# A two-layer relational graph attention kernel: float32 key products and twelve row buffers in the preparation, query numbers of 16 groups gathered by GpSimd

## The chip, the cores and the metric

The kernel runs on one core of a Trainium2 chip. The metric is the device time of one execution in microseconds (us); lower is better. The engines are TensorE (PE; PEld is its weight load), VectorE (DVE), ScalarE (ACT), GpSimd (POOL) and SyncE (SP, which here only issues DMAs). Each engine works through its own row of instructions in order, and DMAs can be issued from SP, ACT and POOL.

## What is computed

Two layers of relational graph attention, a residual and a layer norm. There are 3125 nodes of 768 features, 53125 edges sorted by destination, and 3 relations.

```python
def rgat_conv(x, W, q, k, b, src, dst, etype, heads, out_ch, n_nodes):
    xr = jnp.einsum('nd,rdf->rnf', x, W)
    oi = xr[etype, dst]
    oj = xr[etype, src]
    qi = oi @ q
    kj = oj @ k
    alpha = jax.nn.leaky_relu(qi + kj, NEG_SLOPE)
    m = jax.ops.segment_max(alpha, dst, num_segments=n_nodes)
    e = jnp.exp(alpha - m[dst])
    z = jax.ops.segment_sum(e, dst, num_segments=n_nodes)
    a = e / (z[dst] + EPS)
    msg = (a[:, :, None] * oj.reshape(-1, heads, out_ch)).reshape(-1, heads * out_ch)
    out = jax.ops.segment_sum(msg, dst, num_segments=n_nodes)
    return out + b
...
h = jax.nn.elu(rgat_conv(x, W1, q1, k1, b1, ...))    # 4 heads of 192
out = layernorm(x + rgat_conv(h, W2, q2, k2, b2, ...))   # 1 head of 768
```

An edge's score needs two numbers a head: the key number of its source row and the query number of its destination row, both for the edge's relation. `W @ k` and `W @ q` give columns that are carried along with W, so that one product of x with the widened W yields rows, key numbers and query numbers.

## The kernel before

The 3125 nodes are 25 blocks of 128. The edges are 25 groups: a group holds the edges of up to 128 consecutive destination nodes, in up to 17 slots of 128 edges (14 in the first).

There are four stages, and in each an order written out by hand: a table of steps (`when(n, f, ...)`) lists which function emits its instructions at which step, and every engine's row follows from it.

*The preparation* (`weights_kq`, psum0 and work0). W1 is loaded as 18 rows of 128 features ("W" 0 to 17, six a relation); each is split into a high half (ACT, L378) and a low half (POOL, or DVE for every third, L379), since the big products take a high and a low half of each factor. For the key and query columns each W row is also needed transposed: for relation 0, PE transposes it (L56); for relations 1 and 2 a transposed copy is loaded ("T" rows, two per pair of W rows). The transposes are split into halves too (tH by ACT, L389; tL by DVE, L390). For each pair m = 0 to 8 of W rows, `product(m)` multiplies them with `kqs` (12 matmuls in `times`), ACT copies the result (sm, L402), PE turns it back, and `place` (DVE: L410, L412, and L416 and L417 twice each) writes the columns into the widened weights `waH`, `waL`, `wbH`, `wbL`. Row buffers are handed out by `Buffers`: seven of them, and the next load on SP's row waits until the oldest is free. The edge lists are loaded by ACT and written to DRAM by POOL meanwhile (`prepare`, driven by `more`).

A *piece* is one of 150 products of phase 1's kind: 18 matmuls of a block of x (its halves `xT`) with 386 or 398 columns of the widened weights, into one bank, which ACT copies (L581) and SP stores into the table `tab1`. Each block has six pieces. Pieces 0 to 7 are emitted inside the preparation, between the products of relations 1 and 2; piece 8 is the first of phase 1.

*Phase 1* (`phase1`, psum1 and work1) has the other 142 pieces, one a step, from step 2 on (step n is piece n + 6). Beside them it prepares each group's edges, loads and halves the blocks of x, splits W2 (its rows loaded on POOL's row, L745, into one shared row), and computes each group's query numbers `pall`: `s_load1` loads the group's destination numbers to all partitions (SP), `q_load1` the block's query numbers as three bfloat16 parts (SP), `a_q` and `a_oh` compare (DVE), `a_q2` picks by 17 small matmuls (PE), `a_q3` multiplies and sums (DVE). For the last four groups this stands after the last piece.

*Phase 2* gathers each slot's rows of `tab1` (POOL, L468), forms scores, maxima and weighted sums, and makes the second table; it reads `pall`. *Phase 3* does the second layer and the layer norm.

Of the kernel before, what the change touches and what calls it, by code (L numbers as in the profile page):

```python
# [109 lines left out]
def kernel(  # L110
# [54 lines left out]
    xb_d = dram.tile([NP + P, D], F32, name="xb_d")  # L165
    q1_d = dram.tile([NP + P, H1 * R * 3], BF, name="q1_d")
    w2_d = dram.tile([R * DT * P, 2 * D], F32, name="w2_d")

# [45 lines left out]
    class Buffers:  # L214


        def __init__(self):
# [4 lines left out]
            self.spare = list(range(6)) + [7]  # L222
            self.at = {}
            self.go()

        def __getitem__(self, key):
            return share[self.at[key]][:, :D]

# [120 lines left out]
    def weights_kq(buf, work, psum, kqr, kqs, split, piece, rows_out, more):  # L349

        V.memset(kqs.bitcast(F32), 0.0)
        kq = kqr.rearrange("p t s h -> p t (s h)")
        V.tensor_copy(kqs[:, :, 0:8], kq)
        V.tensor_sub(kqs[:, :, 8:16], kq, kqs[:, :, 0:8].bitcast(F32))

# [7 lines left out]
        def turn(m):  # L363
            r, t = divmod(2 * m, DT)
            made = parts[m] = []
            if r == 0:
                for i in range(2):
# [5 lines left out]
                    made.append(pt)  # L373
            for c in range(2):
                i = 2 * m + c
                hi, lo = (w[:, :, :F1] for w in heads(t + c, r))
                own = buf["W", i].rearrange("p (h f) -> p h f", h=H1)
                S.copy(hi, own)  # L378
                (V if i % 3 == 2 else G).tensor_sub(lo, own, hi.bitcast(F32))  # L379
                buf.free("W", i)  # L380
            for i in range(2):
                hi, lo = (work.tile([P, DT // 2, 2 * P], F32R, name=f"t{n}", bufs=4) for n in "HL")
                if r == 0:
                    to = [t.rearrange("p f (c n) -> p c f n", c=2) for t in (hi, lo)]
                    raw = made[i][:, :, :DT // 2 * P].rearrange("p c (f n) -> p c f n", f=DT // 2)
                else:
                    to = hi, lo
                    raw = buf["T", 2 * m + i].rearrange("p (f n) -> p f n", f=DT // 2)
                S.copy(to[0], raw)  # L389
                V.tensor_sub(to[1], raw, to[0].bitcast(F32))  # L390
                if r > 0:
                    buf.free("T", 2 * m + i)
                made[i:i + 1] = [(hi, lo)]

        prod = {}

        def product(m):
            r, t = divmod(2 * m, DT)
            pk = psum.tile([P, 512], F32, name="bank", bufs=2)[:, :2 * P]
            times(pk, kqs, parts.pop(m))  # L400
            sm = work.tile([P, 2 * P], F32, name="sm", bufs=2)
            S.copy(sm[:16], pk[:16, :2 * P])  # L402
            prod[m] = r, t, sm

        def place(r, t, sm):
            pb = psum.tile([P, 2, 512], F32, name="pt", bufs=2)[:, 0, :]
            for c in range(2):
                T.transpose(pb[:, c * 16:(c + 1) * 16], sm[:16, c * P:(c + 1) * P], ident[:16, :16])
            g = work.tile([P, 2, 16], F32, name="g16", bufs=2)
            V.tensor_copy(g, pb[:, :32].rearrange("p (c k) -> p c k", c=2))  # L410
            w = work.tile([P, 2, 8], F32, name="w8", bufs=2)
            V.tensor_add(w, g[:, :, 0:8], g[:, :, 8:16])  # L412
            k, o = divmod(r, WHOLE)
# [5 lines left out]
        def placed(m):  # L419
            place(*prod.pop(m))  # L420
# [11 lines left out]
        placed(1)  # L432
        split(0)
        placed(2)
        split(1)
        for r in range(1, R):
            m = 3 * r
            for j in range(4):
                piece()
                rows_out(1)  # L440
                if j < 3:
                    turn(m + j)
                if j > 0:
                    product(m + j - 1)
                if j > 1:
                    placed(m + j - 2)
                if r == 1:
                    more(1)
            placed(m + 2)

# [128 lines left out]
    def d_row(o, q, b, p, po):  # L579
# [4 lines left out]
        if p == len(PIECES1) - 1:  # L584
            q1s = q.tile([P, H1 * R, 3], BF, name="q1s", bufs=2)
            split3([q1s[:, :, i] for i in range(3)], po[:, HW:HW + H1 * R], q, [P, H1 * R])
            nc.sync.dma_start(q1_d[b * P:(b + 1) * P, :], q1s.rearrange("p k s -> p (k s)"))

    def stretches(rows, at_, a, e):
# [11 lines left out]
    def phase1(pre, work, psum, left, due, more):  # L601
# [14 lines left out]
        def a_index2(b):  # L616
# [7 lines left out]
            if b in first_rows:  # L624
                V.tensor_scalar(rfirst[:, first_rows[b], :], ridx[:, b, :], NP * R - 1, None, op0=ALU.min)
            V.tensor_copy(rel[:, b, :], pT[:, 2 * c:3 * c])

        counts = work.tile([32, 32], F32, name="counts", bufs=1)
# [54 lines left out]
        def a_oh(b):  # L683
            s = st[b]
            s["oh"] = work.tile([P, SL, R * 3], F32, name="oh", bufs=2)
            V.tensor_tensor(s["oh"], rel[:, b, :, None].to_broadcast([P, SL, R * 3]),
# [51 lines left out]
        def w_load(i):  # L738
# [5 lines left out]
            for p, at, n in feature_rows(t):  # L744
                G.dma_start(w2[i][p:p + n], l2["W"][r, at:at + n, :])  # L745

        def w_split(i):
# [10 lines left out]
            if r < WHOLE:  # L758
                (G if i >= 4 else nc.sync).dma_start(w2_d[i * P:(i + 1) * P, :].rearrange("p (s f) -> p s f", s=2), hl.bitcast(F32))

# [13 lines left out]
        S0 = 10  # L774
        when(8, pad_rows)
        for b in range(NB):
            c = S0 + 5 * b
# [22 lines left out]
        for i in range(R * DT):  # L800
            when(6 * (2 + i), w_load, i)
            when(6 * (2 + i) + 2, w_split, i)
        for p, (r, f, n) in enumerate(((0, 0, HW), (0, HW, D - HW), (1, 0, HW), (1, HW, D - HW))):
            when(TAIL + 4 * p + 5, second_weights, r, f, n)
# [726 lines left out]
    with tc.manual_schedule():  # L1531
        with tc.tile_pool(name="share", bufs=1) as pool:
# [5 lines left out]
            with tc.tile_pool(name="wbuf", bufs=1) as wbuf:  # L1538
                weights[0] = [wbuf.tile([P, DT, WA], F32R, name=f"wa{s}") for s in "HL"]
                with tc.tile_pool(name="wrest", bufs=1) as wrest, tc.tile_pool(name="pre", bufs=1) as pre:  # L1540
# [16 lines left out]
                    with tc.tile_pool(name="work0", bufs=1) as work, tc.tile_pool(  # L1557
                        name="psum0", bufs=1, space=PSUM
                    ) as psum:

                        buf = Buffers()
# [3 lines left out]
                        kqs = work.tile([P, DT, P], F32R, name="kqs")  # L1565
                        banks[:] = [psum.tile([P, 512], F32, name=f"po{i}") for i in range(2)]
# [572 lines left out]
```

## Time and profile before

| what | us |
|---|---|
| median of 3 runs | 1765.43 (1759.7 to 1765.5) |
| the profiled execution, its own time | 1765.7 |
| its span, first to last instruction | 1763.9 |
| start to the first piece | 20.96 |
| first piece to piece 8 (rest of the preparation) | 44.74 |
| phase 1 (142 pieces) | 465.1 |
| from there on (phases 2 and 3) | 1233.1 |

A row of the timeline is: start, length (both us), engine, line, operation, what it writes and reads, shapes, count if equal instructions were put together, and in brackets the idle time before it and what ended that. A row of groups is: line, engine, operation, tiles, shapes, count, then busy us and mean ns of one, then idle time before. "SPq" and "ACTq" are DMA issues on these engines' rows.

### The profile page before, as it was taken

To read this page: it belongs to the slowest core of one execution; us is meant where nothing else is said; L and a number is where in the kernel's file an instruction comes from. 1 tells how busy PE (TensorE), PEld (TensorE's weight loads), DVE (VectorE), ACT (ScalarE), POOL (GpSimd) and SP (SyncE) were. 2 spreads that over 40 slices of the span, in tenths; PEclk is the share of its full clock that TensorE was granted. 3 is DMA by queue.
4 is the path that set the end of the run, shared out by engine and by line. 5 is a ranking of instruction groups with operands and counts; after the bars stand their busy time and mean duration, and the time that the engine had idled before them with its cause. 6 is when DMAs were issued, how large, how long until landed. Compare 5 with 4: busy or idle time off the path is not lost. (4 is left out here: it accounts for less than half of the span.)

```text
span 1763.9 us, 38699 instructions
## 1 busy us (share of the span) xinstructions
PE 1648.9 (93%) x14093; PEld 1282.5 (73%) x14093; DVE 1116.9 (63%) x3911; ACT 438.0 (25%) x805; POOL 901.3 (51%) x907
## 2 busy tenths in 40 slices
PE   8999999999993899999999999939999999999996
PEld 8999999999992688888888888825444444444443
DVE  7566667566525666666677777455666666666663
ACT  6222222211210122121221112212333333333331
POOL 4100000000006777777777777057777777777760
PEclk9999999999996899999999999969999999999998
DMA  8576766656577999999999999469999999999970
GB/s 271 177 243 218 217 224 231 199 171 209 187 266 266 322 350 359 354 349 348 347 345 347 342 349 343 131 218 317 340 339 335 341 336 334 337 337 341 340 274 20
DMA packets 169367, 501.55 MB, mean 284 GB/s; under 512 B 39890, under 2 KB 82489, under 8 KB 169166
## 3 DMA queue, kind: packets, MB, share of 16 engines
q0 software_dynamic: 70832, 343.91, 55.1%
q1 hardware_dynamic: 90104, 144.97, 24.8%
q10 hardware_dynamic: 8230, 10.10, 1.7%
q8 instruction: 113, 1.85, 0.4%
q14 instruction: 88, 0.72, 0.1%
HBM read 414.04 MB, written 89.63 MB: 286 GB/s over the span
## 5 line engine op out<-in xcount | busy, mean ns | idle before, releaser
L468 POOL DMA_INDIRECT extra<-ftab,ridx x296 | 301.6, 1019 | 94.4 <-issue 52.7
L53 PE MATMUL po<-waH,hT 128*128 128x386 f32 (+1 forms) x1200 | 326.2, 346 | 1.4 <-DVE hT L1031 0.7
L53 PE MATMUL po<-waH,xT 128*128 128x386 f32 x1104 | 294.6, 343 | 0.9 <-ACT xT L255 0.4
L468 POOL DMA_INDIRECT share<-ftab,ridx x209 | 211.5, 1012 | 68.9 <-issue 41.0
L53 PEld LDWEIGHTS po<-waH,hT 128*128 128x128 f32 x1200 | 216.6, 189 | 4.8 <-DVE hT L1031 1.1
L53 PE MATMUL D<-extra,AT 128*128 128x256 f32 (+1 forms) x600 | 211.4, 504 | 5.3 <-ACT AT L1399 5.3
L53 PEld LDWEIGHTS po<-waH,xT 128*128 128x128 f32 x1104 | 203.9, 190 | 1.4 <-DVE xT L256 0.8
L53 PE MATMUL po<-waL,hT 128*128 128x386 f32 (+1 forms) x600 | 203.0, 338 | 0.0
L53 PE MATMUL po<-waL,xT 128*128 128x386 f32 x552 | 188.3, 341 | 3.1 <-DVE wbH L416 3.0
L53 PEld LDWEIGHTS D<-extra,AT 128*128 128x128 f32 x600 | 113.9, 196 | 69.6 <-issue 48.3
L581 ACT COPY share<-po 128x386 f32<-128x386 f32 x150 | 72.3, 482 | 368.9 <-PE po L53 296.4
L53 PE MATMUL acc<-waL,marks 128*32 128x386 f32 (+1 forms) x860 | 151.9, 489 | 0.0
L53 PE MATMUL po<-wbH,xT 128*128 128x386 f32 (+1 forms) x552 | 147.5, 341 | 0.9 <-DVE g L410 0.9
L53 PE MATMUL acc<-waH,marks 128*32 128x384 f32 (+1 forms) x828 | 140.4, 493 | 0.7 <-DVE marks L1321 0.7
L53 PE MATMUL acc<-extra,marks 128*32 128x386 f32 (+1 forms) x564 | 129.5, 487 | 0.0
L468 POOL DMA_INDIRECT waL<-ftab,ridx x108 | 107.9, 999 | 33.6 <-issue 25.3
L53 PE MATMUL acc<-extra,sel 128*32 128x193 f32 x2736 | 122.9, 332 | 2.3 <-DVE sel L940 2.3
L468 POOL DMA_INDIRECT waH<-ftab,ridx x103 | 103.7, 1007 | 31.4 <-issue 25.3
L53 PEld LDWEIGHTS po<-waL,hT 128*128 128x128 f32 x600 | 113.3, 189 | 0.0
L53 PE MATMUL acc<-share,marks 128*32 128x384 f32 (+1 forms) x456 | 109.7, 487 | 0.0
L745 POOL DMA_DIRECT2D share<-in_L_gnn_W_dram x24 | 12.8, 538 | 188.5 <-DVE w2j L756 117.1
L53 PEld LDWEIGHTS acc<-extra,sel 128*32 128x32 f32 x2736 | 86.5, 111 | 30.4 <-issue 4.9
(286 smaller groups left out, 2990.9 us busy)
## 6 DMA issues: line engine op xcount, KB each, us to landing
ftab<-share SPq DMA_DIRECT2D x150, 193.0 KB
ftab<-r SPq DMA_DIRECT2D x50, 386.0 KB
sT<-dr_d SPq DMA_DIRECT2D x23, 544.0 KB
xb_d<-share SPq DMA_DIRECT2D x25, 384.0 KB
ftab<-y SPq DMA_DIRECT2D x100, 96.0 KB
share<-xb_d SPq DMA_DIRECT2D x25, 384.0 KB
share<-in_x_dram SPq DMA_DIRECT2D x24, 384.0 KB
out_dram<-share SPq DMA_DIRECT2D x24, 384.0 KB
```

Source lines behind the costliest of these rows:

```text
L53: return self.add(self.engine.matmul(to, weights, moving, **more), to, moving)
L468: return G.indirect_dma_start(out=to, out_offset=None, in_=tab, in_offset=_index(i[:, j:j + 1]), bounds_check=NP * R - 1, oob_is_err=False)
L581: S.copy(o[:, :HW], po[:, :HW])
L745: G.dma_start(w2[i][p:p + n], l2["W"][r, at:at + n, :])
```

## The change

1. *Key products in float32.* `kqs` holds the key and query vectors in 32 columns of float32 (24 are zero) in place of 128 columns of halves. `times` multiplies the transposed rows as they are: 12 matmuls of 32 x 128, which write the four groups of 32 output rows in turn (two feature halves times two W rows). The halves of the transposed rows go. For relation 0 one copy a part remains, half of them on ACT and half on DVE; for relations 1 and 2 the loaded "T" rows are read in place, and are let go after the product. `place` adds up two of the four groups.
2. *Order in the preparation.* `product(m)` stands right behind its `turn(m)`, and `placed` one piece after it; `split(0)` (x's first halves) stands inside `turn(2)`, which takes W row 5 ahead of row 4.
3. *Twelve row buffers*: five more, in work0.
4. *Query numbers by gather.* For 16 groups (b < 20, not every fifth) the six functions above are not emitted. In their place DVE computes each edge's row number (`qi`, two small operations), and POOL gathers four float32 numbers for each edge from a new DRAM tensor `q1r_d`, one indirect DMA a slot, 269 in all, from step 13 on. DVE copies and SP stores each block's query numbers to it. `pall` is set to 0 once, by POOL.
5. *W2.* Its loads are issued from ACT's row in place of POOL's; the split rows are stored from SP's row two steps later (eight of twelve were on POOL's row).
6. `oh` has one buffer in place of two.

```diff
+            self.rows = [t[:, :D] for t in share] + more
+            self.spare = list(range(6)) + [7] + list(range(len(share), len(self.rows)))
...
     def times(to, a, parts):
-        n = 0
-        for i, hl in enumerate(parts):
-            for t in hl:
-                for f in range(3):
-                    T.matmul(to, a[:, 3 * i + f, :], t[:, f, :], start=(n == 0), stop=(n == 2 * DT - 1))
-                    n += 1
+        for f in range(DT // 2):
+            for i, t in enumerate(parts):
+                for c in range(2):
+                    o = 32 * (2 * i + c)
+                    T.matmul(to[o:o + 32, :P], a[:, DT // 2 * i + f, :], t[:, f, c * P:(c + 1) * P], start=(f == 0),
+                             stop=(f == DT // 2 - 1))
...
-            for c in range(2):
+            for i in range(2):
+                if r == 0:
+                    to = work.tile([P, DT // 2, 2 * P], F32, name="t", bufs=4)
+                    (V.tensor_copy if i else S.copy)(
+                        to.rearrange("p f (c n) -> p c f n", c=2),
+                        made[i][:, :, :DT // 2 * P].rearrange("p c (f n) -> p c f n", f=DT // 2))
+                    made[i] = to
+                else:
+                    made.append(buf["T", 2 * m + i].rearrange("p (f n) -> p f n", f=DT // 2))
+            for c in (range(2) if m != 2 else (1, 0)):
...
+                if i == 5:
+                    split(0)
                 buf.free("W", i)
-            for i in range(2):
-                hi, lo = (work.tile([P, DT // 2, 2 * P], F32R, name=f"t{n}", bufs=4) for n in "HL")
...
-                S.copy(to[0], raw)
-                V.tensor_sub(to[1], raw, to[0].bitcast(F32))
...
                 if j < 3:
                     turn(m + j)
+                    product(m + j)
                 if j > 0:
-                    product(m + j - 1)
-                if j > 1:
-                    placed(m + j - 2)
+                    placed(m + j - 1)
...
+        def by_gather(b):
+            return b < GB - 1 and b % 5 != 4
+
+        def q_gather(b, j):
+            n = (b + 1) * P * R
+            G.indirect_dma_start(out=pall[:, b, j, :], out_offset=None, in_=q1r_d[:n, :],
+                                 in_offset=_index(st[b]["qi"][:, j:j + 1]), bounds_check=n - 1, oob_is_err=False)
...
-                G.dma_start(w2[i][p:p + n], l2["W"][r, at:at + n, :])
+                nc.scalar.dma_start(w2[i][p:p + n], l2["W"][r, at:at + n, :])
...
-            for n, f in zip(k, (s_load1, q_at, q_load1, a_q, a_oh, a_q2, a_q3)):
-                when(n, f, b)
+            if by_gather(b):
+                for j in range(slots(b)):
+                    when(max(6 * b + 9, c + 3) + j * 7 // SL, q_gather, b, j)
+            else:
+                for n, f in zip(k, (s_load1, q_at, q_load1, a_q, a_oh, a_q2, a_q3)):
+                    when(n, f, b)
```

On PE, in the preparation ahead of the first piece, there stood before (bank is the result of a key product or of filling matmuls, tH and tL the halves of the transposed rows, pt the place for turning, po the bank of a piece):

```order
L53 MATMUL bank<-fident 128x128 x6
L56 MATMUL pt<-fident,sm 128x16 x2
L53 MATMUL bank<-tH,kqs 128x256 x3
L53 MATMUL bank<-tL,kqs 128x256 x3
L53 MATMUL bank<-tH,kqs 128x256 x3
L53 MATMUL bank<-tL,kqs 128x256 x3
L56 MATMUL pt<-fident,sm 128x16 x4
L53 MATMUL po_140<-waH,xT 128x386
```

and now:

```order
L53 MATMUL bank<-fident 128x128 x6
L56 MATMUL pt<-fident,sm 128x128
L53 MATMUL bank<-t,kqs 32x128 x12
L56 MATMUL pt<-fident,sm 128x128 x2
L53 MATMUL po_147<-waH,xT 128x386
```

Each key product is 12 matmuls of a quarter of the output rows and half the columns, and its result is turned back by one transpose in place of two.

On DVE, from the first transposed rows to the first key columns, there stood before (waL is the low half of W rows, g and w the columns on their way to the weights):

```order
L390 TENSOR_TENSOR tL<-pt,tH 128x2x3x128 x2
L379 TENSOR_TENSOR waL<-share,waH 128x4x192
L390 TENSOR_TENSOR tL<-pt,tH 128x2x3x128 x2
L379 TENSOR_TENSOR waL<-share,waH 128x4x192
L390 TENSOR_TENSOR tL<-pt,tH 128x2x3x128 x2
L410 COPY g_286<-pt 128x32
L412 TENSOR_TENSOR w_288<-g_286 128x16
```

and now:

```order
L377 COPY t<-pt 128x2x3x128 x2
L388 TENSOR_TENSOR waL<-share,waH 128x4x192
L377 COPY t<-pt 128x2x3x128
L388 TENSOR_TENSOR waL<-share,waH 128x4x192
L258 TENSOR_TENSOR xT<-share,xT 128x768
L410 COPY g_282<-pt 128x32
L412 TENSOR_TENSOR w_284<-g_282 128x16
```

Three copies stand where six subtractions stood, and the low half of x's first block has moved ahead of the first key columns.

On POOL, from the end of the edge list's stores to phase 2, there stood before (ed_d and dr_d are the edge lists in DRAM, w_d the split W2, ftab the first table):

```order
L279 DMA ed_d<-e 125x425
L745 DMA share<-in_L_gnn_W_dram 128x768 x4
L745 DMA share<-in_L_gnn_W_dram 64x768 x2
L759 DMA w_d<-w2hl 128x1536
L745 DMA share<-in_L_gnn_W_dram 64x768 x2
L759 DMA w_d<-w2hl 128x1536
```

and now:

```order
L281 DMA dr_d<-share 125x425
L281 DMA ed_d<-e 125x425
L838 MEMSET pall 128x1700
L640 DMA pall<-q1r_d,qi 128x4 x269
L465 DMA share<-ftab_62,rfirst 128x772 x9
```

All loads and stores of W2 have left POOL's row, and the 269 gathers stand alone between the edge lists and the row gathers of phase 2.

More of the change, by code (lines that the diff above doesn't have):

```diff
@@ L226, in __getitem__ @@
         def __getitem__(self, key):
-            return share[self.at[key]][:, :D]
+            return self.rows[self.at[key]]
         def free(self, *key):
@@ L398, in product @@
             r, t = divmod(2 * m, DT)
-            pk = psum.tile([P, 512], F32, name="bank", bufs=2)[:, :2 * P]
+            pk = psum.tile([P, 512], F32, name="bank", bufs=2)
             times(pk, kqs, parts.pop(m))
-            sm = work.tile([P, 2 * P], F32, name="sm", bufs=2)
-            S.copy(sm[:16], pk[:16, :2 * P])
+            if r > 0:
+                for i in range(2):
+                    buf.free("T", 2 * m + i)
+            sm = work.tile([P, P], F32, name="sm", bufs=2)
+            S.copy(sm, pk[:, :P])
             prod[m] = r, t, sm
@@ L1559 @@
                     ) as psum:
-                        buf = Buffers()
+                        ahead = work.tile([P, 5, D], F32, name="ahead", bufs=1)
+                        buf = Buffers([ahead[:, i, :] for i in range(5)])
                         kqr = work.tile([P, DT, 2, H1], F32, name="kqr", bufs=1)
```

50 lines of the change are left out of this document (25 added, 25 removed).

## The prediction

> **What bounds the kernel now.** I read the page first, then the busy time of each engine in three stretches, then the order of time inside the first of them. The page says that TensorE (PE) works nearly all the time, and that GpSimd (POOL) has almost nothing to do in the first third.
>
> ```profile
> PE 1648.9 (93%) x14093; PEld 1282.5 (73%) x14093; DVE 1116.9 (63%) x3911; ACT 438.0 (25%) x805; POOL 901.3 (51%) x907
> PE   8999999999993899999999999939999999999996
> POOL 4100000000006777777777777057777777777760
> ```
>
> The stretches are: until the first table product of layer 1, the rest of the preparation, and phase 1. The columns are the length, each engine's busy time, the granted clock, the DMA share and GB/s.
>
> ```profile
> 0.00:20.96 20.96, 17.48 (x121) 16.54 (x121) 11.78 (x32) 12.37 (x18) 8.10 (x12) 1.00 0.82 283
> 20.96:65.70 44.74, 39.79 (x229) 38.02 (x229) 33.90 (x64) 24.07 (x39) 17.93 (x14) 0.92 0.64 206
> 65.70:530.80 465.10, 465.10 (x2915) 460.97 (x2915) 276.89 (x1016) 93.66 (x176) 19.40 (x36) 1.00 0.67 216
> ```
>
> In phase 1 PE is busy for 465.10 of 465.10 us: only work taken off PE shortens it. In the preparation PE waits and does other work: its 8 pieces (a piece is 18 matmuls into one bank) would need far less than 44.74 us. The rows that show where the rest goes:
>
> ```profile
> 20.96 0.44 PE L53 MATMUL po<-waH,xT 128*128 128x386 f32 x1 [0.44 <-ACT xT L255]
> 25.50 0.48 ACT L581 COPY share<-po 128x386 f32<-128x386 f32 x1 [0.92 <-PE po L53]
> 28.48 0.51 PE L53 MATMUL bank<-tH,kqs 128*128 128x256 f32 x3
> 29.90 0.34 PE L53 MATMUL po<-waH,xT 128*128 128x386 f32 x1
> ...
> 39.33 0.17 DVE L417 TENSOR_TENSOR waL<-w,waH 128x8 fp32r<-128x8 f32 x1
> 42.11 3.68 DVE L417 TENSOR_TENSOR waL<-w,waH 128x8 fp32r<-128x8 f32 x1
> 42.43 3.32 POOL L379 TENSOR_TENSOR wbL<-share,wbH 128x768 fp32r<-128x768 f32 x2
> 45.93 0.66 PE L53 MATMUL po<-waL,xT 128*128 128x386 f32 x1 [2.96 <-DVE wbH L416]
> ...
> 65.70 0.41 PE L53 MATMUL po<-wbH,xT 128*128 128x386 f32 x1 [0.88 <-DVE g L410]
> ```
>
> Piece 0 runs from 20.96 to 25.50, piece 8 (the first of phase 1) starts at 65.70. One key product takes PE from 28.48 to 29.90, 1.42 us. And one subtraction of eight columns on VectorE (DVE), 0.17 us at 39.33, took 3.68 us at 42.11, until two POOL subtractions were through; piece 4 waited 2.96 us for it. After that wait the clock is low:
>
> ```profile
> 45.93:52.11 6.18, 6.18 (x19) 6.18 (x20) 4.32 (x5) 3.41 (x5) 1.73 (x1) 0.51 0.92 292
> ```
>
> 6.18 us at 0.51 of the clock lose 6.18 x 0.49 = 3.0 us. The stall costs 6.0 us in all.
>
> **The change: the preparation.** A piece is worked out from phase 1. The score products that stand among its pieces:
>
> ```profile
> 433.09 0.34 PE L53 MATMUL po<-wbH,xT 128*128 128x398 f32 x1
> 433.27 0.59 PE L53 MATMUL pq<-q,sT 128*128 128x36 bf16 x17
> 433.71 0.42 PE L53 MATMUL po<-waH,xT 128*128 128x386 f32 x1
> ...
> L53 PE MATMUL pq<-q,sT 128*128 128x36 bf16 x357 | 12.4, 179 | 0.0
> ```
>
> A group's 17 score products move the next piece from 433.27 to 433.71, 0.44 us; 357 of them are 21 groups. So 142 pieces take 465.1 - 21 x 0.44 = 455.9 us, 3.21 us each.
>
> The key products go from 12 matmuls of 256 columns to 12 of 128 columns in four groups of 32 output rows. Two rows bound them: phase 2's float32 matmuls of that tile, and float32 matmuls over the whole array.
>
> ```profile
> 808.14 3.47 PE L53 MATMUL acc<-share,sel 128*32 128x193 f32 x80
> 12.28 1.50 PE L53 MATMUL bank<-fident 128*128 128x128 f32 x12
> ```
>
> The first gives 3.47/80 = 43 ns for 193 columns, so 12 x 43 x 128/193 = 0.35 us; the second 1.50 us, no gain at all. I take 0.5, by the first row, whose type and tile it is, with something for getting in and out. "TensorEngine Tiling (Array Packing)" in the Trainium skill, section Key Properties, has a rule against this: changing the tiling mode drains the TensorE. The trace shows no such change around so short a product; the allowance above covers it only in part, and the upper bound in full.
>
> The halves of the transposed weights go altogether: no cast and no subtraction for the loaded ones, one copy in their place for the first relation.
>
> ```profile
> L390 DVE TENSOR_TENSOR tL<-share,tH 128x768 fp32r<-128x768 f32 x12 | 13.5, 1157 | 1.9 <-ACT tH L389 1.8
> L389 ACT CAST tH<-share 128x768 fp32r<-128x768 f32 x12 | 9.7, 831 | 2.8 <-DMA share<-in_w_t_dram 2.8
> L389 ACT CAST tH<-pt 128x768 fp32r<-128x768 f32 x6 | 4.7, 803 | 1.3 <-PE pt L56 1.3
> L379 POOL TENSOR_TENSOR waL<-share,waH 128x768 fp32r<-128x768 f32 x8 | 14.7, 1844 | 15.5 <-ACT waH L378 15.5
> ```
>
> Until piece 0, ScalarE (ACT) loses three casts of 0.80 us, 2.4 us; and piece 0 took 4.54 us, 1.3 more than a piece needs, because its last columns came late. So piece 0 could end 3.7 us earlier. But POOL keeps its subtractions, and three of them (for W rows 4, 6 and 7, 1.84 us each, 5.5 together) now stand beside DVE's nine two-input operations for the first three pairs of key columns. If DVE waits for all three, piece 0 ends 5.5 - 3.7 = 1.8 us later. I take 1 us earlier, nearer to the blocked end, since the row at 42.11 is this very pair. "SBUF — State Buffer" in the Trainium skill, section Who interferes with whom, says the same more generally: a DVE instruction with two SBUF inputs and a GpSimd one that reads SBUF exclude each other for a whole instruction. The row at 42.11 agrees.
>
> From the end of piece 0 to piece 8 it was 65.70 - 25.50 = 40.2 us. Now: 7 pieces x 3.21 = 22.5, six products x 0.5 = 3.0, six transposes of their results x 0.3 = 1.8, together 27.3. That is 12.9 us less: 5.5 of it from the products, 6.0 from the stall, the rest from transposes and the wait of 0.88. The stall goes because the product that fed it (the last of a relation) now stands ahead of piece 3 and not behind it, so that its columns can be placed as soon as piece 3 ends, before POOL's next subtraction. What is late next there is POOL's subtraction for W row 10, which now stands behind the five stores of the edge list on POOL. If it holds piece 4 as the old wait did, the 6.0 come back. The preparation gives 1.0 + 12.9 = 13.9 us; at the least nothing (12.9 - 1.8 - 6.0 - 6 x 1.0 is just below it), at the most 3.7 + 12.9 = 16.6.
>
> Five more row buffers let the loads run on. The DMA view of the first 66 us, in forty slices:
>
> ```profile
> GB/s 0 240 276 342 408 415 408 402 400 248 235 225 21 89 124 206 249 302 239 325 333 227 343 284 287 350 372 310 262 318 266 344 95 5 115 0 92 38 0 65
> DMA packets 7936, 15.28 MB, mean 232 GB/s; under 512 B 2375, under 2 KB 3729, under 8 KB 7931
> ```
>
> 15.28 MB at the 400 GB/s of the first slices are 38 us, and piece 8 would start at 24.5 + 27.3 = 51.8. The loads hide, with 14 us to spare.
>
> **The change: phase 1.** PE loses 16 of the 21 groups: 16 x 0.44 = 7.0 us (by the busy time, 12.4/21 = 0.59 each, 9.4). DVE loses their comparisons, products and sums and gains one small copy a block and two operations a group; at 276.89 of 465.10 us that is worth nothing. ACT takes W2's 18 loads from POOL; its copies wait for PE most of the time, so I cost them at nothing:
>
> ```profile
> L581 ACT COPY share<-po 128x386 f32<-128x386 f32 x142 | 68.5, 483 | 364.4 <-PE po L53 291.9 <-issue 53.5 <-DMA T<-ed_d 5.5
> L468 POOL DMA_INDIRECT extra<-ftab,ridx x224 | 229.7, 1025 | 72.4 <-issue 36.0 <-PE po L53 13.1 <-PE acc L53 11.2
> ```
>
> If a W2 load waited for its buffer, the copies behind it would be late, and PE after two pieces; the buffer is let go four pieces ahead. POOL gains 269 gathers. The second row gives (229.7 + 72.4)/224 = 1.35 us for one of phase 2's: 363 us. They can start at step 13, 131 pieces before the end: 131 x 3.21 = 420 us. They fit, with 57 us to spare. Nothing in phase 1 reads what they bring; the one new wait there is DVE's for one of seven index tiles, which holds the splits of x queued behind it (and so PE) only if POOL is some seven groups late. At the end SP has one store more behind the old one; the first row gather at 534.34 waits for the old ones, 0 to 0.4 us.
>
> ```profile
> 532.47 0.34 SPq L587 DMA_DIRECT2D q_d<-q1s  x1
> 534.34 1.12 POOL L468 DMA_INDIRECT share<-ftab,rfirst  x1 [113.32 <-DMA q_d<-q1s]
> ```
>
> Phases 2 and 3 keep their instructions and only move. The sum, against the profiled execution's own 1765.7 us (span 1763.9; the median is 1765.43, the same within 0.3 us): 1765.7 - 13.9 - 7.0 = 1744.8, given as 1745.
>
> **The rivals.** *The gather queue overflows* (slower). Past 420/269 = 1.56 us a gather, the last ones hold POOL when the first row gather should go out, and each 0.1 us more costs 27 us; it is slower than before by over 0.5% from about 1.67 us. At 1.75 it gives 1745 + 269 x 0.19 = 1796. For it: these gathers stand beside other DVE work than phase 2's, and fetch 16 bytes a row, which no row here shows. Against it: 1.35 us beside a busy DVE. "SBUF — State Buffer" in the Trainium skill, section SBUF: two separate sides, describes a cause: GpSimd cannot write its descriptors while DVE runs an operation in a two-port mode. By that rule phase 1 could stretch them; the mean of 1025 ns in phase 2 shows little of it. Chance 0.10.
>
> *The waits come back* (no change). POOL's subtractions hold DVE before piece 0 for over 3 us, so that PE starts at half clock, and again before piece 4: two stalls of 6.0 us, 1745 + 12 = 1757. The 3.68 us row speaks for it, the earlier products against it. Chance 0.16.
>
> *The column groups do not overlap*: products of 1.5 us, 6 x 1.0 = 6 more, 1751. Chance 0.08.
>
> **How the numbers follow.** The forecast keeps 0.66. The range reaches from both gains at their most (1765.7 - 16.6 - 9.4 = 1739.7, and about 4 us for the spread of the runs shown) to the second rival with 2 us: 1736 to 1759. The overflow lies outside. A measurement here can tell about 0.5%, 8.8 us. Faster: forecast and third rival, 0.74; the same: 0.16; slower: 0.10.
>
> **What would show it.** In the changed profile piece 0 should end near 24.5 and piece 8 start near 52, with key products of about 0.5 us and no PE wait of 3 us between; phase 1 should last about 458 us with PE still busy throughout; POOL should show gathers at about 1.35 us each and be idle well before phase 2. I am wrong if piece 8 starts after 60, if PE idles inside phase 1, or if the row gathers of phase 2 start more than 4 us after PE's last piece.

## The result, and the profile after

| | median us | runs |
|---|---|---|
| kernel before | 1764.24 | 6 (1759.7 to 1768.22) |
| changed kernel | 1750.51 | 6 (1749.61 to 1756.03) |

The ratio is 0.9931, 95% interval 0.9914 to 0.9949: 12 us faster (9 to 15). The forecast was 1745, 20.9 us below the profiled execution of before; the profiled execution after has a span of 1747.7, 16.2 below 1763.9. So the sign held, the time lies inside 1736 to 1759, and part of the gain is missing: a quarter by these two executions, a third by the medians (13.7 us). Later runs show something larger that the prediction did not have: on some other chips the same change makes the kernel 10% slower. Ratios here and below go by the fast executions; two of the six of "gathers alone" on chip 4 were in a slower state and are left out.

The page of the changed kernel, the engines' shares and POOL's slices; POOL is now busy from the third slice of forty on:

```profile
PE 1632.6 (93%) x13920; PEld 1264.5 (72%) x13920; DVE 1072.8 (61%) x3872; ACT 425.5 (24%) x790; POOL 1178.6 (67%) x1145
POOL 4277777777507777777777776067777777777750
```

The stretches of the changed kernel: to piece 0, piece 0, to piece 8, phase 1. The columns are those of the prediction (length, busy time and count of PE, PEld, DVE, ACT, POOL, granted clock, DMA share, GB/s):

```profile
0.00:17.65 17.65, 14.24 (x153) 12.50 (x153) 9.07 (x21) 10.44 (x16) 8.58 (x12) 1.00 0.92 334
17.65:25.44 7.79, 5.29 (x22) 4.43 (x26) 6.89 (x21) 1.16 (x2) 3.32 (x2) 0.78 0.92 357
25.44:55.96 30.52, 29.18 (x276) 26.08 (x276) 16.00 (x38) 12.40 (x24) 13.79 (x12) 1.00 0.66 212
55.96:516.34 460.38, 457.32 (x2643) 455.01 (x2643) 246.19 (x991) 93.68 (x176) 297.80 (x274) 1.00 0.67 200
```

Piece 8 starts at 55.96, 9.7 us earlier than before (65.70). Phase 1 lasts 460.4 us, 4.7 less than 465.1. The remaining 1.8 of the 16.2 came behind phase 1, where the spread between executions is about as large. Piece 0 should take 3.2 us and took 7.8. The timeline of the changed kernel shows why, and shows the second surprise at 66 us:

```profile
15.50 1.86 POOL L388 TENSOR_TENSOR waL<-share,waH 128x768 fp32r<-128x768 f32 x1 [2.01 <-ACT waH L387]
15.95 1.44 DVE L412 TENSOR_TENSOR w<-g 128x16 f32<-128x16 f32 x1
17.42 0.17 DVE L416 CAST waH<-w 128x8 fp32r<-128x8 f32 x1
17.65 0.44 PE L53 MATMUL po<-waH,xT 128*128 128x386 f32 x1 [0.66 <-DVE waH L416]
18.16 1.69 POOL L388 TENSOR_TENSOR waL<-share,waH 128x768 fp32r<-128x768 f32 x1 [0.80 <-ACT waH L387]
18.23 1.65 DVE L412 TENSOR_TENSOR w<-g 128x16 f32<-128x16 f32 x1
19.82 1.66 POOL L388 TENSOR_TENSOR waL<-ahead,waH 128x768 fp32r<-128x768 f32 x1
19.92 1.60 DVE L416 CAST waH<-w 128x8 fp32r<-128x8 f32 x1
21.57 0.44 PE L53 MATMUL po<-waH,xT 128*128 128x386 f32 x1 [2.50 <-DVE waH L416]
25.37 0.90 PE L53 MATMUL bank<-ahead,kqs 128*32 128x128 f32 x24
...
29.56 0.86 PE L53 MATMUL bank<-share,kqs 128*32 128x128 f32 x24
30.35 0.33 PE L56 MATMUL pt<-fident,sm 128*128 128x128 f32 x1
...
50.21 0.41 PE L53 MATMUL bank<-share,kqs 128*32 128x128 f32 x4 [0.41 <-DMA share<-in_w_t_dram]
51.10 0.85 PE L53 MATMUL bank<-share,kqs 128*32 128x128 f32 x20 [0.47 <-DMA share<-in_w_t_dram]
55.96 0.44 PE L53 MATMUL po<-wbH,xT 128*128 128x386 f32 x1 [0.46 <-DVE w L412]
...
57.39 0.33 SPq L252 DMA_DIRECT2D xr<-in_x_t_dram  x1
65.30 0.83 ACT L257 CAST xT<-xr 128x768 fp32r<-128x768 f32 x1 [5.24 <-DMA xr<-in_x_t_dram]
66.03 0.86 ACT L578 COPY share<-po 128x386 f32<-128x386 f32 x2
68.26 0.42 PE L53 MATMUL po<-wbH,xT 128*128 128x398 f32 x1 [2.43 <-DVE q1f L586]
```

Three rows of DVE (1.44, 1.65, 1.60 us for operations of 0.17) end each within 0.1 us of a POOL subtraction's end. PE waits 0.66 and 2.50 us for them, and the rest of piece 0 runs at a low clock: it was 0.57 from 21.57 to 25.44, and 7.79 us at a mean of 0.78 lose 1.7. At 65.30 ACT's cast of the third block of x has waited 5.24 us for its load, two copies of finished pieces stand behind it, and PE waits 2.43 us; the row names DVE's last small copy, which itself came late.

The gathers of the changed kernel, as a group, the first one, and the first row gather of phase 2:

```profile
L640 POOL DMA_INDIRECT pall<-q1r_d,qi x269 | 294.2, 1094 | 95.7 <-issue 91.1 <-DMA pall<-q1r_d,qi 3.0 <-DVE c L212 0.6
...
90.24 1.11 POOL L640 DMA_INDIRECT pall<-q1r_d,qi  x1 [13.97 <-issue]
519.75 1.00 POOL L465 DMA_INDIRECT share<-ftab,rfirst  x1 [53.60 <-DMA q1r_d<-q1f]
```

(294.2 + 95.7)/269 = 1.45 us a gather; without the 13.97 us that POOL waited for the first, it is 1.40. They end at 466, 53.6 us before POOL is needed.

### The profile page after: what moved, and what is told of

It is laid out like the page before. It is cut to its first block, busy times and chain, and to the rows that moved or that the text cites. A ratio compares the mean times of both kernels' runs of the same rounds, so it can differ in the third digit from the quotient of the medians.

```text
span 1747.7 us, 38741 instructions
## 1 busy us (share of the span) xinstructions
PE 1632.6 (93%) x13920; PEld 1264.5 (72%) x13920; DVE 1072.8 (61%) x3872; ACT 425.5 (24%) x790; POOL 1178.6 (67%) x1145
## 5 line engine op out<-in xcount | busy, mean ns | idle before, releaser
L640 POOL DMA_INDIRECT pall<-q1r_d,qi x269 | 294.2, 1094 | 95.7 <-issue 91.1
```

The source lines that it names most:

```text
L640: G.indirect_dma_start(out=pall[:, b, j, :], out_offset=None, in_=q1r_d[:n, :], in_offset=_index(st[b]["qi"][:, j:j + 1]), bounds_check=n ...
```

## The experiments

Twelve runs were spread over four chips, and the chips fall into two classes. The kernel before takes 1764 us on the first comparison's chip and on chip 1, and 2001, 2004 and 2002 us on chips 4, 5 and 13. Each ratio is to the kernel before on the same chip, with its interval.

| run | chip | median us | ratio (95%) |
|---|---|---|---|
| preparation alone | 4 | 1994.87 | 0.9962 (0.9946 to 0.9977) |
| gathers alone | 4 | 2202.39 | 1.0989 (1.0948 to 1.1029) |
| no lock | 4 | 2201.13 | 1.0988 (1.0954 to 1.1022) |
| x ahead | 4 | 2205.46 | 1.1011 (1.0986 to 1.1035) |
| both edits | 1 | 1746.51 | 0.9905 (0.9886 to 0.9924) |
| gathers alone, again | 1 | 1757.71 | 0.9966 (0.9953 to 0.9979) |
| 20 groups gathered | 1 | 1782.34 | 1.0107 (1.0088 to 1.0127) |
| seven buffers | 5 | 2215.85 | 1.1059 (1.1021 to 1.1097) |
| W2 on GpSimd | 5 | 2159.18 | 1.0799 (1.0773 to 1.0826) |
| 18 groups, both edits | 5 | 2224.03 | 1.1097 (1.1061 to 1.1132) |
| changed kernel, again | 5 | 2203.07 | 1.1002 (1.0981 to 1.1024) |
| preparation with both edits, no gathers | 13 | 1988.76 | 0.9927 (0.9911 to 0.9943) |

### The two halves of the change

Preparation alone: points 1 to 3 of the change (lines 215 to 450, the buffers), nothing else. Gathers alone: points 4 to 6. In place of a diff, the line that tells them apart:

```diff
 preparation alone
+                        buf = Buffers([ahead[:, i, :] for i in range(5)])
 gathers alone
+            if by_gather(b):
+                for j in range(slots(b)):
+                    when(max(6 * b + 9, c + 3) + j * 7 // SL, q_gather, b, j)
```

> The kernel before with the preparation of the change alone (float32 key products in four column groups, no halves of the transposed weights, twelve row buffers, the new places of the steps); all 21 groups keep their score products and W2's loads stay on GpSimd. If the parts simply add: piece 8 at 56.0 as in the changed kernel (before 65.7), the wait of 2.4 us for the third block of x at two or three pieces into phase 1 is there too, phase 1 from piece 8 to the last piece 465.1 + 2.4 = 467.5, and the time 7 to 8 us below the kernel before. If the gathers' table stores on the SyncE queue are what makes that wait (theory B), it is absent here and the time is about 9.7 us below.

> The kernel before with the query gathers alone (16 groups by GpSimd, W2's loads on ScalarE's queue, the stores of W2's halves on SyncE's); the preparation is the old one. If the parts add: piece 8 stays at 65.7, no wait inside phase 1, phase 1 lasts 465.1 - 7.2 = 457.9 us, GpSimd's gathers take 1.45 us each and end about 476, 45 us before the last piece; time 7 to 9 us below the kernel before. If the gathers cost phase 1 something that the shorter preparation hides (theory B), PE waits inside phase 1 and the gain is under 5.

> The kernel before with the query gathers alone, again. On a chip that runs the changed kernel in 1750 us: piece 8 at 65.7, PE busy through phase 1, which lasts 457.9 us instead of 465.1, time 7 to 9 us below the kernel before (0.995 to 0.996). Rival (what was seen on the last chip is a property of the gathers and not of that chip): PE waits in phase 1 for ScalarE's copies, which wait for the stores of the table, and the ratio is above 1.05.

The preparation alone gave 2001.39 - 1994.87 = 6.5 us by the medians (0.0038 of 2001 is 7.6 by the ratio), about as expected if the parts add. In its trace piece 8 came at 60.81 and not at 56.0; of these 4.8 us 1.0 was there at the start of piece 0 (18.68), 1.6 came from a wait for a transposed row (1.99 us in place of 0.41), and 1.7 from the clock behind that wait (0.57 for 3.98 us). The late block of x is there too: ACT waits 4.06 us for its load, but PE only 0.53 where theory A said 2.4, so these two theories stay undecided. The gathers alone gave 6.5 us (1764.2 - 1757.71) on chip 1, a little under the 7 to 9: piece 8 at 67.48 in the old preparation (65.70 in the trace of before), phase 1 of 458 us as expected, and no wait of PE above 0.4 us in it. The two add up to 13 or 14, which is what the whole change gave (12 to 14), though they come from two chips. On chip 4 the gathers alone cost 200 us; that has a section of its own below.

### The lock before piece 0, and the late block of x

No lock: three subtractions go from POOL to DVE. X ahead: one load goes from step 2 of phase 1 to the end of the preparation.

```diff
 no lock
-                (V if i % 3 == 2 else G).tensor_sub(lo, own, hi.bitcast(F32))
+                (V if i % 3 == 2 or i in (4, 6, 7) else G).tensor_sub(lo, own, hi.bitcast(F32))
 x ahead
+                if r == R - 1 and j == 3:
+                    x_load(2, share[3][:, :D])
...
-                when(t, d_load, b)
+                if b > 2:
+                    when(t, d_load, b)
```

> The changed kernel with the subtractions for W rows 4, 6 and 7 on VectorE instead of GpSimd, so that no GpSimd subtraction stands beside VectorE's operations for the first three pairs of key columns. Theory A (GpSimd's subtractions hold VectorE, and that is what made piece 0 end at 25.4 with a wait of 2.5 us and half clock behind it): VectorE's additions and casts there take 0.17 us each, no PE wait over 1 us before the end of piece 0, which ends near 21, and piece 8 starts near 52, time 3 to 5 us below the changed kernel. Theory B (the loads of W and its transpose set the pace of the preparation): piece 0 ends near 21 as well, but PE then waits for the transposed rows, piece 8 starts at 54 to 56 and the time falls by 0 to 2 us.

> The changed kernel with the load of the third block of x issued at the end of the preparation (into a free row buffer) instead of behind the bias and residual loads at the start of phase 1. Theory A (the wait of 2.43 us at 65.8 is ScalarE's cast of that block standing in front of its copies of finished pieces until the load lands): the wait is gone, phase 1 lasts 458 us, time 2.0 to 2.6 us below the changed kernel. Theory B (VectorE's new copy of the query numbers, which the wait is put down to, or the order of the split, causes it): a wait of 1 to 2.4 us stays and the time falls by under 1 us.

The gains of these two are lost in the 10% that the gathers cost on chip 4, but their first 80 us are not, and they can be set against each other. The timeline of "no lock":

```profile
17.79 0.17 DVE L412 TENSOR_TENSOR w<-g 128x16 f32<-128x16 f32 x1
18.00 0.17 DVE L416 CAST waH<-w 128x8 fp32r<-128x8 f32 x1
...
18.23 0.44 PE L53 MATMUL po<-waH,xT 128*128 128x386 f32 x1
21.71 0.86 PE L53 MATMUL bank<-ahead,kqs 128*32 128x128 f32 x24
...
47.08 0.41 PE L53 MATMUL bank<-share,kqs 128*32 128x128 f32 x4 [0.97 <-DMA share<-in_w_t_dram]
47.95 0.85 PE L53 MATMUL bank<-share,kqs 128*32 128x128 f32 x20 [0.46 <-DMA share<-in_w_t_dram]
52.79 0.44 PE L53 MATMUL po<-wbH,xT 128*128 128x386 f32 x1 [0.46 <-DVE w L412]
65.28 0.67 PE L53 MATMUL po<-wbH,xT 128*128 128x398 f32 x1 [2.63 <-DVE q1f L586]
```

With POOL's three subtractions away, DVE's operations take 0.17 us, piece 0 runs from 18.23 to 21.7 without a wait, and piece 8 starts at 52.79. The timeline of "x ahead", which keeps the lock:

```profile
22.92 0.69 PE L53 MATMUL po<-waH,xT 128*128 128x386 f32 x1 [2.48 <-DVE waH L416]
58.13 0.44 PE L53 MATMUL po<-wbH,xT 128*128 128x386 f32 x1 [0.46 <-DVE w L412]
...
64.86 0.84 ACT L257 CAST xT<-share 128x768 fp32r<-128x768 f32 x1 [2.64 <-PE po L53]
```

The 2.48 us and the late piece 8 are there, and the wait behind piece 8 is gone: ACT's cast now waits for PE's work and not for a load. Both theories A hold in these rows; what the edits are worth in time, chip 4 cannot show. Only 0.5 us of the first gain came back as a longer wait for the transposed rows (0.97 + 0.46 in place of 0.41 + 0.47). The version with both edits went to chip 1:

> The changed kernel with both edits: W rows 4, 6 and 7 subtracted on VectorE, and the third block of x loaded at the end of the preparation. If what the two took was really on the path to the end: piece 8 near 52.5 (56.0 in the changed kernel), no wait for x behind it, the last piece's end 5 to 6 us earlier than 516.3, time 5 to 6 us below the changed kernel on a chip that runs it in 1750 us, so 1744 to 1746, a ratio to the kernel before of 0.989. Rival: phase 2 cannot start earlier than GpSimd's gathers end (466 us), which is far off, so a smaller gain would mean that the loads of x or W2 wait in their turn: a wait of over 1 us in phase 1. If the chip is like the last one, where the gathers of phase 1 held the stores of the table, the ratio is 1.09 to 1.10 whatever these edits do.

Its timeline, piece 8 and the first row gather:

```profile
52.35 0.44 PE L53 MATMUL po<-wbH,xT 128*128 128x386 f32 x1 [0.46 <-DVE w L412]
...
513.61 1.00 POOL L467 DMA_INDIRECT share<-ftab,rfirst  x1 [55.61 <-DMA q1r_d<-q1f]
```

The row gathers start at 513.61, 6.1 us before those of the changed kernel, as expected (5 to 6). The time, 1746.51, is 4.0 below the changed kernel's (measured on another chip of the same class), a little less: from the first row gather to the end of the span this execution took 1231.1 us (1744.7 - 513.6), the changed kernel's 1228.0. Phases 2 and 3 have the same instructions in both, and took 1229.6 in the kernel before, so I take the 6.1 as the better number for the two edits.

### How full GpSimd's row is

```diff
-            return b < GB - 1 and b % 5 != 4
+            return b < GB - 1
```

> The changed kernel with all 20 of the groups up to the last one gathered instead of 16: 4 x 17 = 68 gathers more, no score products of theirs on PE. Theory A (GpSimd's queue is the limit that the rival of the prediction named): 337 gathers at 1.45 us are 489 us from about 76 on, so they end near 565, about 48 us behind the row gathers' start in the changed kernel (519.75); phase 1 is 4 x 0.44 = 1.8 us shorter, PE idles behind its last piece, and the time is 40 to 50 us above the changed kernel. Theory B (the rate follows the room: the 1.45 us hold waits that vanish when the queue is full, 1.30 each): 337 x 1.30 = 438, end at 514, and the time falls by 1 to 2 us.

The gathers of this run as a group, and from its timeline the first row gather, which follows the last query gather at once, and PE's wait for the rows:

```profile
L640 POOL DMA_INDIRECT pall<-q1r_d,qi x337 | 361.9, 1074 | 116.5 <-issue 110.4 <-DMA pall<-q1r_d,qi 4.0 <-DVE share L747 0.9
...
556.74 0.99 POOL L465 DMA_INDIRECT share<-ftab,rfirst  x1 [0.30 <-issue]
572.57 0.80 PE L56 MATMUL pa<-fident,al 128*32 128x128 f32 x3 [47.26 <-DMA extra<-ftab,rfirst]
```

(361.9 + 116.5)/337 = 1.42 us, against 1.45 with 269: the rate hardly falls when the row is full. The row gathers start 37.0 us later than in the changed kernel and PE waits 47.26 us where it waited 10.5; the time is 31.8 us above. Theory A holds, with a smaller excess than the 40 to 50 expected. The mechanism of the slower rival is real, but 16 groups stay clear of it on this chip.

### Buffers, W2's loads, 18 groups

These three went to chip 5 with the changed kernel itself as a control.

```diff
 seven buffers
-                        buf = Buffers([ahead[:, i, :] for i in range(5)])
+                        buf = Buffers([])
 W2 on GpSimd
-                nc.scalar.dma_start(w2[i][p:p + n], l2["W"][r, at:at + n, :])
+                G.dma_start(w2[i][p:p + n], l2["W"][r, at:at + n, :])
 18 groups, on top of both edits
-            return b < GB - 1 and b % 5 != 4
+            return b < GB - 1 and b % 10 != 9
```

> The changed kernel with the seven row buffers of the kernel before instead of twelve. Theory A (the five more buffers let W's rows and its transpose run ahead, and without them the loads set the pace): PE waits for rows of the transposed W ahead of most of the six products, 1 to 3 us each, piece 8 starts at 62 to 68 instead of 56, and the time is 6 to 12 us above the changed kernel, near the kernel before with the gathers alone (1757). Theory B (PE's pieces set the pace and the earlier products were enough): piece 8 within 1 us of 56, the time within 1 us of the changed kernel.

> The changed kernel with W2's 18 loads issued by GpSimd again, where they now stand between the gathers. Theory A (GpSimd's queue runs some groups behind the order of the steps, so W2's rows come late, ScalarE's cast of them stands in front of its copies, and PE waits): PE waits in phase 1 of 1 to 5 us several times, 10 us or more in all. Theory B (GpSimd keeps up with the steps, being idle for 54 us at the end of phase 1): no wait over 1 us, gathers end 10 to 20 us later than 466, time within 2 us of the changed kernel.

> The version with both edits (subtractions for W rows 4, 6, 7 on VectorE, third block of x loaded early) and 18 groups gathered instead of 16. By the rate of 1.44 us a gather, 34 gathers more end 49 us later, near 506, 7 us ahead of the row gathers at 513; PE has 2 x 0.44 = 0.9 us less. Theory A (they fit): 0.5 to 1.5 us below the version with 16. Theory B (the last gathers lag, as the 20 groups did): the row gathers start later than 514 and the time is 2 to 10 us above it.

> The changed kernel as it is, on the same chip as the three others of this call. On a chip like the first: ratio to the kernel before 0.993, piece 8 near 56, wait for x of 2.4 us. On a chip like the one on which the gathers alone gave 1.099: ratio 1.09 to 1.10.

Seven buffers: its preparation answers. The timeline:

```profile
37.89 1.45 PE L53 MATMUL bank<-share,kqs 128*32 128x128 f32 x20 [1.82 <-DMA share<-in_w_t_dram]
...
53.91 0.41 PE L53 MATMUL bank<-share,kqs 128*32 128x128 f32 x4 [2.34 <-DMA share<-in_w_t_dram]
56.04 1.50 PE L53 MATMUL bank<-share,kqs 128*32 128x128 f32 x20 [1.72 <-DMA share<-in_w_t_dram]
67.73 0.44 PE L53 MATMUL po<-wbH,xT 128*128 128x386 f32 x1 [0.46 <-DVE w L412]
```

Piece 8 starts at 67.73, in the control at 57.36: without the five buffers PE waits for transposed rows and the new preparation has no gain left. Theory A holds. The other two are inconclusive on their questions, since on this chip phase 1 is governed by something else. W2 on GpSimd is 44 us faster than the control there, where it was expected to be slower or equal; in it, ACT's waits for W2's rows were small (5.5 us in three waits between 80 and 510 us). 18 groups are slower than 16 (1.1097 against 1.1002), although that version also has both edits.

### Where the gathers cost 10%

In the control on chip 5 phase 1 runs from 57.36 to 705, 648 us in place of 460. The row gathers start 3.4 us behind its end and POOL's last query gather was out at 602.5, so POOL's row is not the limit. PE is busy for 499 us and idle for 148, and the granted clock is 0.88 in place of 1.00. PE waits for ACT, and ACT, as the waits of phase 1 show (engine and tile, what was waited for, us, times, longest), for "remote", a release that this view puts down to no instruction:

```profile
ACT share L578 <- remote: 198.5, 18, 30.4
ACT share L578 <- PE po L53: 175.9, 56, 6.6
```

The same waits in the changed kernel on its first chip:

```profile
ACT share L578 <- PE po L53: 239.7, 88, 4.9
...
ACT share L578 <- DMA ftab<-share: 18.9, 7, 2.7
```

What a copy needs is a finished piece and a row whose last store to the table has landed. One stall of the control on chip 5, in its timeline and in the DMA view of 242 to 256 us:

```profile
237.40 0.70 SPq L252 DMA_DIRECT2D share<-in_x_t_dram  x1
257.08 0.48 ACT L578 COPY share<-po 128x386 f32<-128x386 f32 x1 [24.09 <-remote]
257.59 0.32 SPq L580 DMA_DIRECT2D ftab<-share  x1
257.62 0.69 PE L53 MATMUL po<-waH,xT 128*128 128x386 f32 x1 [18.17 <-issue]
...
DMA packets 342, 0.02 MB, mean 2 GB/s; under 512 B 342, under 2 KB 342, under 8 KB 342
q0 software_dynamic: 342, 0.02, 10.4%
```

For 14 us the only packets of the core are those of POOL's gathers (queue 0). It looks as if the gathers starved the queues of SP and ACT, but the trace says otherwise. SP issued nothing between 237.40 and 257.59, since its next DMA stores what the waiting copy makes, ACT issued nothing after 227.2, and the packets of all they had issued had moved by 240. The gathers went at their usual pace: 342 packets are 10.7 gathers of 32 packets, and a gather has 32 in the first chip's trace too.

What the copy waited for stands in the trace's semaphore records. ACT's wait for the store was over at 232.53. The copy's own wait is for the semaphore that the last matmul of a piece raises; its piece ended at 232.32, and the raise that ends the wait is recorded at 257.06, when PE had been through the next piece as well and stood idle since 239.45. All 18 "remote" waits (198.5 us) end within 0.1 us behind a raise of that semaphore, and none at a recorded landing of a store. In the control 34 of phase 1's 142 copies start more than 3 us behind the end of their piece, the latest 31.6 us; in the changed kernel on its first chip one does (3.4), and in the preparation alone on chip 4 none (2.2 at most). So by these records PE's signal reaches ACT late while the gathers run, and PE in turn stands still for want of the copy. One caution: the traces of chips 4, 5 and 13 hold fewer semaphore records than those of the other class (17686 against 33264 for the changed kernel, 19486 for the preparation alone against 29363 for the kernel before), so a release that is missing there proves nothing.

The preparation alone on chip 4 has no query gathers, and its phase 1 takes 465.9 us (60.81 to 526.72), as before; but what follows, where the row gathers run, takes 1472 us in place of 1233. The windows from 600 to 1100 us, of the preparation alone on chip 4 and of the kernel before on the first chip:

```profile
600.00:1100.00 500.00, 467.11 (x5061) 385.92 (x5061) 294.14 (x844) 84.21 (x184) 319.76 (x316) 0.99 0.90 294
```

```profile
600.00:1100.00 500.00, 497.76 (x5898) 430.29 (x5900) 350.99 (x996) 99.83 (x217) 377.82 (x370) 1.00 0.97 347
```

With points 4 to 6 of the change the ratio on chip 4 is 1.0989, and with points 1 to 3 alone 0.9962, so the 10% comes with points 4 to 6. Which of them it is was tried in part: with W2's loads back on POOL's row 1.0799 is left, and two groups more cost 1%. That it is the gathers is therefore likely and not shown by itself, and why PE's signal comes late, and only on these chips, is open. "DMA: Bandwidth & Descriptors" in the Trainium skill, section Queues, rings and completion order, says that a DMA engine takes turns between the queues that have work, packet by packet; the 14 us with packets of one queue alone do not speak against that, since the other queues had nothing to hand over.

One version should be safe on both classes, the new preparation with both edits and without the gathers:

```diff
 preparation alone
+                (V if i % 3 == 2 or i in (4, 6, 7) else G).tensor_sub(lo, own, hi.bitcast(F32))
...
+                if r == R - 1 and j == 3:
+                    x_load(2, share[3][:, :D])
...
-                when(t, d_load, b)
+                if b > 2:
+                    when(t, d_load, b)
```

> The new preparation alone (no query gathers, W2's loads on GpSimd as in the kernel before) with both edits: W rows 4, 6 and 7 subtracted on VectorE and the third block of x loaded at the end of the preparation. Theory A (the preparation's gain is worth the same on any chip, and only the gathers make the difference between the chips): on a chip where the kernel before takes 1764 us, piece 8 near 52.5 instead of 65.7, no wait behind it, 11 to 14 us below the kernel before, ratio 0.992 to 0.994; on one where it takes 2001 us, the 7.6 us of the preparation alone plus 4 to 5 us, ratio 0.993 to 0.995. Theory B (the early loads collide there as the gathers' did): PE waits for loads in the preparation or phase 1 and the ratio is 0.997 or more.

It gave 0.9927 on chip 13, where the kernel before takes 2001.98 us: 13 us. Piece 8 is at 52.66, and PE waits for nothing else until phase 1's end. Theory A holds, with a ratio just past the expected 0.993. On chip 1's class the version with both edits and the gathers is the best that was run (0.9905); where the gathers cost 10%, this one is.

## Why the prediction was right, and its gain too large

*Piece 0 (step "1 us earlier"): mis-sized inside its bounds.* It ended at 25.44, as late as before (25.50). The two ends of the bound were 1.8 later and 3.7 earlier; the free end is right ("no lock": 21.7), and the blocked end was too late by 1.9. The 1 us earlier was called nearer to the blocked end, but it is the middle of the two, although the row at 42.11 of before had already shown the whole price of such a pair. The half of the second rival that concerns this place came true in substance: DVE was held for 4.2 us in all, PE waited 2.50 us, inside piece 0 and not before it, and the clock behind the wait was 0.57. One thing was not in it: a DVE cast with a single input was held as well (19.92, 1.60 us). The page cited there, "SBUF — State Buffer" in the Trainium skill, has it, in the section Who interferes with whom: casts can enter a mode that takes both ports. That the cast was held agrees, with 1.60 us beside 0.17; in which mode it ran, no row shows.

*The stall before piece 4: right in its outcome.* The columns were not placed ahead of POOL's subtraction, as I had it: it held an addition again (2.43 us at 35.19). But PE did not wait for them, and the 6.0 us stayed saved.

*The key product (0.5 us): mis-counted.* It took 0.8 (29.56 to 30.35). My row gave 43 ns a record, and I multiplied it by 12 instructions; the profile writes 24 records for 12 float32 matmuls, as it wrote 12 for the six filling matmuls in the row at 12.28. With 24 the sum is 24 x 43 x 128/193 = 0.68 us, and with something for getting in and out, 0.8. The column groups do overlap (36 ns a record, against 125 over the whole array), so the third rival fell. From piece 0's end to piece 8 it was 30.52 us in place of 27.3. By the starts in the timeline, the six products took 5.1 in place of 3.0, the seven pieces 23.4 in place of 22.5, and the six transposes only 0.6 in place of 1.8; the other 1.3 are two waits for the last transposed rows (0.9) and one for the last columns (0.46), which the sum did not have. "The loads hide with 14 us to spare" was wrong there: by bandwidth they do, but with buffers let go only by the products, the last rows were asked for at 44.

*Phase 1 (458 us): right in the work, wrong in "busy throughout".* PE was busy for 457.3 us. The wait of 2.43 was in no term. Piece 8 came 10 us earlier, and the block of x did not keep up: its cast started 9.3 us behind the start of piece 8 (65.30), before 7.4. Its load stood behind two others on SP's row, and "x ahead", which issues it earlier, has no such wait. By my own mark (PE idles inside phase 1) the prediction was wrong at this place.

*The gathers (1.35 us, break-even 1.56): 1.45, and the rest as said.* From their real start at 90.24 to the row gathers at 519.75, the break-even is 429.5/269 = 1.60, to be held against 1.40. Row gathers started 3.4 us behind PE's last piece, as before (3.5).

*The tail and phases 2 and 3:* forecast 0, measured 1.8 us in favour, within what executions differ by.

In sum, of 20.9 us, 4.2 went before piece 8 and 2.3 in phase 1, and 1.8 came back behind it. That the total came this near is in part luck: the 1.8 us and the transposes, priced 1.2 too high, cover part of what was missed. What the prediction lacked altogether is the slower case on the other chips: the rival that I named (POOL's row overflows) is not how it happens. The trace of before came from a chip of the other class, and nothing in it could show the difference.

## What to carry to other kernels

Before moving work off DVE's or POOL's path, list which POOL operations that read SBUF will stand beside DVE's short ones on the critical path, and price each pair at the whole POOL operation. When a stage starts earlier, look for the load that its first consumer needs and whether an in-order engine would wait for it in front of finished work. Moving work to a stream of small gathers had a price of 10% that the first chip did not show: try such a change on several. And before blaming a queue for standing still, look whether anything was issued to it.

## What the runs showed of the hardware

- A float32 matmul of these shapes is two records in the profile (12 key matmuls are 24, six filling ones 12). With four column groups of 32 used in turn, a record of 128 columns takes 36 ns, against 125 ns over the whole array: the groups run beside each other.
- A POOL subtraction holds DVE's casts of one input as well as its operations of two: 1.60 us in place of 0.17.
- Chips differ by 13% on the kernel before (1764 against 2002 us). Phase 1 without gathers takes 465.9 us on chip 4 and 465.1 on the first; what follows takes 1472 against 1233 us.
- With points 4 to 6 of the change, phase 1 takes 648 us on chip 5 in place of 460, and ACT's copies start up to 31.6 us behind the end of their piece, when PE's raised semaphore is recorded.
- On that chip, with W2's loads between the gathers on POOL's row, the kernel was 44 us faster (1.0799 against 1.1002). Why was not tried.
